# The order of the query tiles in the last attention chunk of a transformer block

## The chip, the cores and the metric

The kernel runs on one core of a Trainium2 chip. The metric is the device time of one execution in microseconds (us), less is better. The engines are called TensorE (PE in the profile; PEld is its weight loading), VectorE (DVE), ScalarE (ACT), GpSimd (POOL) and SyncE (SP, which here only issues DMAs).

## The reference

One layer: causal attention with 16 heads of 32, then a feed forward with the signs of its weights, each followed by a residual sum and a layer norm. Cut to what matters:

```python
# x: (2, 1024, 512) f32
qkv = einsum('bsd,ed->bse', x, w_qkv) + b_qkv            # 3 x 512 columns
scores = q @ k.T / sqrt(32) + causal                      # per batch and head
out = softmax(scores) @ v                                 # back to (2, 1024, 512)
x = layernorm(x + einsum('bsd,ed->bse', out, w_out) + b_out)
hidden = relu(einsum('bsd,hd->bsh', x, sign(up_w)) * up_scale)      # 2048 columns
x = layernorm(x + einsum('bsh,dh->bsd', hidden, sign(down_w)) * down_scale * output_scale)
```

All is float32. Where precision allows fast matmuls, operands are split into a high part and a remainder.

## The kernel before

**Chunks and tiles.** A chunk is one batch with four heads (128 columns); there are 2 x 4 = 8 chunks, done one after the other, and the last is batch 1, heads 12 to 15. Within a chunk the 1024 queries are eight tiles of 128. Because of the causal mask tile i has (i + 1) blocks of 128 keys: tile 0 has 1, tile 7 has 8. Every chunk but the last takes its tiles in the order 0 to 7. The last takes them in the order of the list `LAST`. While one chunk's attention runs, the projections of the next chunk (L568 queries and keys, L605 values) are mixed into TensorE's work; the last chunk has no next one. Instead it has the output projection of batch 1, the signs of the feed forward's weights and the first transposes of the feed forward.

**One tile** goes through these steps for its four heads, which are taken four at a time (tiles 0, 1), two at a time (2, 3) or one at a time (4 to 7):
- scores on TensorE (L861) into one of two double banks of PSUM (`sc`, in the profile `d`)
- on VectorE the mask and the negated maximum of a row: one custom instruction per head and a read of its accumulator (L899), or for four heads at once a sum (L881) and a reduction (L891)
- on ScalarE the exponential with its row sum (L914), on VectorE the reciprocal (L926), on GpSimd the multiplication by it (L932)
- transposes of 128x128 blocks on TensorE (L961), up to four into one bank, and a copy of the bank on ScalarE (L506) or VectorE (L508), whichever the planner takes
- products with the values on TensorE (L988), in one group for one or more tiles, into one bank, and a sum with the value bias on VectorE that writes the chunk's columns into `atT` (L1008)

**Which tiles share a value group.** `attend` puts a tile on a list; if the tile is in `TOGETHER` and is not the chunk's last, the list waits for the next tile, otherwise one group is made of all on the list:

```python
TOGETHER = (0, 1, 3, 4, 6)
...
            apart = i == tiles[-1] or at == 0 and i < NQ // 2
            attend(b, e, i, past, i in TOGETHER and not apart)
            past += i + 1
```

In the last chunk `LAST = [0, 1, 2, 7, 6, 5, 4, 3]` gives the groups 0+1+2, 7, 6+5, 4+3.

**Output and first norm.** When all four chunks of a batch have a tile's columns, `output` multiplies them with `w_out` (L1053, four pairs of matmuls, one per chunk), adds on VectorE the residual row (L1064) and takes statistics (L1068, L1072). The residual row is loaded by SP (`rows<-in_x`) into a single buffer, and GpSimd adds the output bias to it (L1047); the next row's load waits until the sum at L1064 has read it. `normalise` then computes the eight inverse deviations of a batch at once on GpSimd (L1082, L1089) and scales its eight tiles on VectorE (L1097).

**Feed forward.** Four blocks of 512 rows. A block needs its rows transposed (L1122) and split into two parts by ScalarE (L1129) and VectorE (L1134) in `xt`. For each of 16 slices f of the hidden columns: eight up matmuls (L1174), relu on ScalarE (L1185), a cast and a remainder on VectorE (L1191, L1196, `hid`), and down products (L1218) for four row tiles. The signs of the weights are taken on ScalarE (L1148), four pieces of 1 MB for each matrix, from the buffer `raw`, which holds one piece, or for two pieces of the down weights from the space of `atT`. The first block is of batch 0 and needs nothing of the last chunk but its space: the hidden slices lie where probabilities were, and the signed down weights where the last chunk's queries and keys were.

**What sets the order.** The program is a list of tasks with a due place each. A planner in the program (`Plan.schedule`) goes through them with costs written down for each task, takes on each engine the ripe task with the smallest place, and so fixes the order on every engine and the buffer of every tile before the program is built. Due places in the last chunk follow from the list: `past` grows by i + 1 with each tile, scores get `at - EAGER` (12 earlier), values `base - 2`, outputs the tile's own begin plus i + 1 + `LAG` (6). Four single banks of PSUM are shared by transposes, value groups, projections and up matmuls, with a limit for each class (`SHARES`). On the chip each engine keeps the planned order and waits on semaphores.

The line that is changed is read here:

```python
        tiles = list(range(NQ))
        if at + 1 == len(chunks):
            tiles = LAST
```

Of the kernel before, what the change touches and what calls it, by code (L numbers as in the profile page):

```python
# [27 lines left out]


TOGETHER = (0, 1, 3, 4, 6)  # L30
LAST = [0, 1, 2, 7, 6, 5, 4, 3]
HURRY = 6.0
PTB = 60

# [247 lines left out]
def kernel(  # L282
# [1025 lines left out]
    for at, (b, e) in enumerate(chunks):  # L1308
# [4 lines left out]
        if at + 1 == len(chunks):  # L1313
            tiles = LAST
        begin, past = {}, base
# [110 lines left out]
```

## Time and profile before

| | |
|---|---|
| median of 3 runs | 757.22 us (756.72 to 757.74) |
| the profiled execution's own time | 758.0 us |
| its span, first to last instruction | 756.2 us |
| granted TensorE clock, mean | 0.999 |
| attention's last chunk, about | 431 to 498 us of the span |
| feed forward, about | 504 us to the end |
| busy in the stretch 480 to 490 us: TensorE, VectorE, ScalarE | 9.58, 6.57, 6.45 us |

The profile is of one execution. Busy time is the union of an engine's instructions; a matmul's end is modelled. In the table of stretches each row gives for one stretch its length and then the busy time and instruction count of each engine. In a timeline each row gives start, length, engine, line, operation, what it writes and reads, shape and count, and in brackets the idle time before it and what ended that.

### The profile page before, as it was taken

Reading aid. Unit: us, or ns where it says so; the run is one execution under the profiler, and the core shown is the slowest. Engines: PE = TensorE matmul, PEld = TensorE weight load, DVE = VectorE, ACT = ScalarE, POOL = GpSimd, SP = SyncE. Lnnn points to the kernel's source line nnn. Section 1 sums busy time; section 2 is a strip of 40 time slices with the busy share of each in tenths; the row PEclk is TensorE's granted clock in tenths of the full one; section 3 lists DMA queues with packets and bytes.
Section 4 is the critical chain, followed back from the end, with each engine's and each line's share of the span. In section 5 each row is a group of like instructions: output and inputs, shape, how many; then the busy total and the mean of one; then the engine's idle time right before and its main releaser. Section 6 shows DMA issues by size and latency. Waiting matters only on the chain.

```text
span 756.2 us, 15485 instructions
## 1 busy us (share of the span) xinstructions
PE 745.9 (99%) x5890; PEld 576.9 (76%) x5890; DVE 479.5 (63%) x1152; ACT 377.4 (50%) x848; POOL 257.0 (34%) x327
## 2 busy tenths in 40 slices
PE   9999999999999999999999999999999999999996
PEld 5668869769757776886977977668787787778885
DVE  2657787787755766887778769744336337335536
ACT  1448776766742755677676667823222222222210
POOL 2416445445535453554544555521001002002000
PEclk9999999999999999999999999999999999999999
DMA  6576446056454225514505534241001001000101
GB/s 185 129 160 149 120 99 141 28 113 155 126 127 112 56 71 112 120 37 100 126 1 114 126 113 154 84 136 74 1 0 57 0 1 56 0 1 1 56 1 55
DMA packets 38216, 62.35 MB, mean 82 GB/s; under 512 B 6144, under 2 KB 18432, under 8 KB 38144
## 3 DMA queue, kind: packets, MB, share of 16 engines
q1 hardware_dynamic: 36912, 60.85, 31.5%
q8 instruction: 46, 0.75, 0.5%
q10 hardware_dynamic: 1232, 0.53, 0.3%
q14 instruction: 26, 0.21, 0.1%
HBM read 24.66 MB, written 4.19 MB: 38 GB/s over the span
## 4 chain that ended last, share of the span: by engine, by line
PE 93%; DVE 4%; SPq 1%; ACT 1%; DMA 0%; issue 0%; ACTq 0%; DVEq 0%
PE s L961 16%; PE s L1174 15%; PE pd L1218 14%; PE s L568 13%; PE d L861 9%; PE s L988 9%; PE s L1053 7%; PE s L605 7%; PE s L769 1%; SPq L524 1%; PE s L1122 1%; DVE small L1264 1%; DVE atT L1247 1%; DVE d L899 1%; PE s L726 1%; ACT probs L914 1%
## 5 line engine op out<-in xcount | busy, mean ns | idle before, releaser
L932 POOL TENSOR_SCALAR probs<-probs,small 128x128 f32<-128x128 f32 (+7 forms) x256 | 189.1, 749 | 233.1 <-DVE small L926 151.2
L914 ACT ACTIVATE probs<-d,small 128x128 f32<-128x128 f32 (+7 forms) x256 | 189.3, 747 | 47.8 <-DVE small L926 18.7
L899 DVE CUSTOM_DVE_ANT_0 d<-d,mask 128x384 f32<-128x384 f32 (+7 forms) x200 | 173.3, 877 | 26.2 <-PE d L861 23.1
L961 PE MATMUL s<-ident,probs 128*128 128x128 f32 x1152 | 161.4, 273 | 1.1 <-DVE probsT L508 0.7
L961 PEld LDWEIGHTS s<-ident,probs 128*128 128x128 f32 x1152 | 135.5, 140 | 32.9 <-issue 23.3
L506 ACT COPY probsT<-s 128x512 f32<-128x512 f32 (+3 forms) x206 | 100.8, 519 | 116.0 <-PE s L961 111.9
L1174 PE MATMUL s<-xt,stacks 128*128 128x512 f32 x512 | 133.1, 400 | 0.0
L1218 PE MATMUL pd<-stacks,hid 128*128 128x512 f32 (+1 forms) x512 | 131.8, 392 | 0.6 <-DVE hid L1191 0.6
L1185 ACT ACTIVATE hf<-s,ups 128x512 f32<-128x512 f32 x64 | 44.0, 688 | 160.3 <-PE s L1174 158.5
L861 PE MATMUL d<-stacks 128*128 128x512 f32 (+3 forms) x368 | 120.8, 423 | 0.9 <-ACT probs L914 0.9
L568 PE MATMUL s<-xT,wqkv 128*128 128x512 f32 x240 | 118.6, 595 | 0.3 <-DMA wqkv<-in_w_qkvT 0.3
L1174 PEld LDWEIGHTS s<-xt,stacks 128*128 128x128 f32 x512 | 94.3, 188 | 23.8 <-issue 1.0
L1218 PEld LDWEIGHTS pd<-stacks,hid 128*128 128x128 f32 x512 | 92.7, 188 | 22.6 <-DVE hid L1191 1.4
L1191 DVE CAST hid<-hf 128x512 fp32r<-128x512 f32 x64 | 27.4, 428 | 121.7 <-ACT hf L1185 121.7
L508 DVE COPY probsT<-s 128x512 f32<-128x512 f32 (+3 forms) x139 | 81.7, 596 | 22.5 <-PE s L961 18.4
L861 PEld LDWEIGHTS d<-stacks 128*128 128x128 f32 x368 | 59.8, 190 | 35.8 <-issue 20.4
L605 PE MATMUL s<-wqkv,xT 128*128 128x128 f32 x512 | 75.5, 276 | 0.0
L605 PEld LDWEIGHTS s<-wqkv,xT 128*128 128x128 f32 x512 | 67.9, 191 | 6.6 <-issue 5.6
L988 PE MATMUL s<-probsT,v 128*32 128x128 f32 x2304 | 68.9, 274 | 0.1
L988 PEld LDWEIGHTS s<-probsT,v 128*32 128x32 f32 x2304 | 61.2, 110 | 10.2 <-DVE small L926 2.7
L1053 PE MATMUL s<-wout,atT 128*128 128x512 f32 x128 | 63.4, 594 | 0.0
L568 PEld LDWEIGHTS s<-xT,wqkv 128*128 128x128 f32 x240 | 39.5, 190 | 19.3 <-issue 17.8
(71 smaller groups left out, 517.6 us busy)
## 6 DMA issues: line engine op xcount, KB each, us to landing
stacks<-wqkv SPq DMA_DIRECT2D x224, 128.0 KB, 2.4
wqkv<-in_w_qkvT SPq DMA_DIRECT2D x22, 256.0 KB, 3.6
xT<-in_xT SPq DMA_DIRECT2D x16, 256.0 KB, 4.4
rows<-in_x SPq DMA_DIRECT2D x16, 256.0 KB, 2.7
raw<-in_up_wT SPq DMA_DIRECT2D x4, 1024.0 KB, 5.1
out<-atT SPq DMA_DIRECT2D x16, 256.0 KB, 2.0
stacks<-wqkv SPq DMA_DIRECT2D x48, 64.0 KB, 2.0
raw<-in_down_wT SPq DMA_DIRECT2D x2, 1024.0 KB, 5.6
```

The costliest lines, as they stand in the source:

```text
L506: nc.scalar.copy(dst, src)
L568: nc.tensor.matmul(of(ps).rearrange("p a b -> p (a b)"), lhsT=of(w)[:, c, n, :], rhs=of(xt)[:, c, t0 : t0 + TB], start=(c == 0), stop=(c = ...
L605: nc.tensor.matmul(of(ps)[:, t, :], lhsT=of(xt)[:, c, t0 + t * P : t0 + (t + 1) * P], rhs=of(w)[:, c, 2, :], start=(c == 0), stop=(c == NC ...
L861: nc.tensor.matmul(of(sc)[:, at0 : at0 + k1 - k0], lhsT=of(st)[:, 0, u, ts(i, P)], rhs=of(st)[:, 1, u, k0:k1], start=True, stop=True,)
L899: lambda _, j=j, some=some: nc.vector.tensor_tensor_reduce(some(), some(), keys(mask[:, S - N :], 0, N), scale=-1.0, scalar=LARGEST, op0=A ...
L914: lambda _, j=j: nc.scalar.activation(keys(of(pr), j, N), keys(of(sc), j, W), AF.Exp, bias=of(nm)[:, j : j + 1], scale=sign, accum_out=of( ...
L932: lambda _, j=j: nc.gpsimd.tensor_scalar(of(pr)[:, j * N : (j + 1) * N], of(pr)[:, j * N : (j + 1) * N], of(sums)[:, j : j + 1], 1.0, ALU. ...
L961: lambda _, k=k, c=c, tp=tp: nc.tensor.transpose(of(tp)[:, k, :], of(pr)[:, c], ident),
L988: nc.tensor.matmul(of(to)[ts(u, HD), n, :], lhsT=of(v)[:, k, ts(u, HD)], rhs=turned(pt, c + k, 1)[0], start=(k == i), stop=(k == 0),)
L1053: lambda _, c=c: nc.tensor.matmul(bank(py), lhsT=of(a)[:, c, :], rhs=of(wout)[:, c, :], start=(c == 0), stop=(c == NC - 1),),
L1174: lambda _, f=f, c=c, n=n, pu=pu: nc.tensor.matmul(of(pu), lhsT=of(up)[:, f // TPB, c, ts(f % TPB, P)], rhs=of(xt)[:, n, c, :], start=(c = ...
L1218: lambda _: nc.tensor.matmul(of(to)[:, d0:d1], lhsT=of(h)[:, ts(t, P)], rhs=of(dn)[:, f // 4, f % 4, d0:d1], start=(f == 0 and n == 0), st ...
```

## The change

One list of eight numbers, the order in which the last chunk takes its query tiles. The rest of the program text is the same.

```diff
 TOGETHER = (0, 1, 3, 4, 6)
-LAST = [0, 1, 2, 7, 6, 5, 4, 3]
+LAST = [2, 7, 6, 5, 4, 3, 1, 0]
 HURRY = 6.0
```

Three things follow from it through the code above. Tiles 0 and 1 go from the chunk's start to its end. The value groups become 2, 7, 6+5, 4+3+1+0. And all due places of the chunk's tasks change, so the planner gives another order to every engine from the chunk's start on: on TensorE up to the first down products of the feed forward, on VectorE until a little later, on ScalarE, GpSimd and SP in the order of exponentials, signs, row sums and loads.

## The prediction

> **What bounds the kernel now.** I read the page's first two parts, then the chain of waits, then TensorE's own waits, then busy time by stretch. The page's busy line and the chain's summary:
>
> ```profile
> PE 745.9 (99%) x5890; PEld 576.9 (76%) x5890; DVE 479.5 (63%) x1152; ACT 377.4 (50%) x848; POOL 257.0 (34%) x327
> PE 93%; DVE 4%; SPq 1%; ACT 1%; DMA 0%; issue 0%; ACTq 0%; DVEq 0%
> ```
>
> TensorE is nearly always occupied and carries 93% of the chain that ended last. So an order of work can only gain what TensorE now idles, and loses whatever new idle time it makes. The view of TensorE's waits shows how little there is:
>
> ```profile
> PE s L726 <- DVE x L722: 1.0, 1, 1.0
> PE d L861 <- ACT probs L914: 0.9, 2, 0.7
> PE s L961 <- DVE probsT L508: 0.7, 1, 0.7
> PE pd L1218 <- DVE hid L1191: 0.6, 2, 0.3
> PE s L568 <- DMA wqkv<-in_w_qkvT: 0.3, 1, 0.3
> PE s L961 <- DVE xT L1064: 0.3, 1, 0.3
> ```
>
> Of these the change can reach 0.7 (L861, at 450.2), 0.7 (L961, at 477.3) and 0.3 (L961, at 489.1). The first lies at the kernel's start, the two on hid in the second half.
>
> The order of instructions says where the change begins and ends. TensorE's first changed instruction starts at 430.95 (the scores of tile 0 before, of tile 2 after, while 10 of the value projections at L605 are still to come). Its first down product (L1218) starts at 508.75 by the chain; from there to the end the order on TensorE is the same in both kernels. Busy time in that stretch, and in the part of it where tiles 7 to 4 are worked through:
>
> ```profile
> core 0: us, PE busy (x) PEld busy (x) DVE busy (x) ACT busy (x) POOL busy (x), PEclk, DMA share, GB/s
> 430.95:508.75 77.80, 75.95 (x741) 55.03 (x741) 57.20 (x142) 50.21 (x103) 35.90 (x42) 1.00 0.34 111
> 443.07:484.20 41.13, 39.59 (x393) 28.86 (x392) 34.36 (x87) 31.48 (x57) 20.23 (x21) 1.00 0.38 129
> ```
>
> TensorE idles 77.80 - 75.95 = 1.85 us in the whole stretch. In the second, VectorE is busy for 34.36 of 41.13: it is next in line.
>
> **What is moved.** Counted from the two orders, TensorE runs the same instructions between those two points: 32 pairs of output projection, 168 attention transposes, 16 transposes for the feed forward, 48 score matmuls, 408 value matmuls, 10 pairs of value projection, 16 up matmuls. Nothing is added or removed, so the change in span is the change in idle time. The value groups (L988) go from tiles 0+1+2, 7, 6+5, 4+3 (24, 32, 52, 36 pairs) to 2, 7, 6+5, 4+3+1+0 (12, 32, 52, 48). What moves is filler: output projections that can run as soon as a group's columns exist. Before, 12 pairs (tiles 0 to 2, 12 x 0.86 = 10.3 us) become ready at 453 and cover tiles 7 and 6. After, 4 pairs (3.4 us) do, then 4 of tile 7, and 16 pairs are left for the end. In return tile 7's scores start beside the last value projections.
>
> **A ledger through the new order.** I walked TensorE's new order from 430.95 with durations of this profile (start to start): 0.109 a transpose, 0.86 a pair of output projection, 0.47 two score matmuls of 512 columns, value groups at 0.029 a matmul; on the others 1.15 a maximum over 1024 keys on VectorE, 1.11 an exponential of 1024 on ScalarE with its accumulator, 0.48 to 0.60 a copy of 512, 1.03 a normalising multiply of 1024 on GpSimd, 1.8 a sign, 0.1 a hand-over. Where it comes out tight:
> - Scores of tile 6, second head: TensorE is there at 448.5. The bank needs tile 7's last exponential, which stands behind a sign on ScalarE (445.5 to 447.3) and ends at 448.4. Slack 0.1.
> - Values of tile 7: at 453.5, last copy 453.4. Slack 0.1.
> - Tile 7's output projection waits 0.1 for its bank (copy on VectorE ends 457.4).
> - Ahead of values 6+5, around 467: a sign on ScalarE (466.4 to 468.2) again stands among the casts of xt, and VectorE's subtraction and two copies follow one another. Waits 0.35 + 0.25 + 0.25 = 0.85.
> - Tile 3's transposes: 0.3 for a copy queued behind a mask on VectorE (479.4), then 0.45 because GpSimd adds tile 5's residual row (1.28 us) between the normalising multiplies of two heads.
> - Last group, 4+3+1+0: copies done at 491.9, TensorE there at 492.3. No wait; it has one up matmul in front and 10 output pairs with 15 up matmuls behind (12 us), which hide the relu, the hid casts and the down weights' signs.
>
> The sum of idle time is 0.1 + 0.85 + 0.75 = 1.7 us against 1.85: -0.15. The same kind of wait is visible before, in ScalarE's timeline, where a sign between two casts made the 0.75 us gap at 477.3:
>
> ```profile
> 475.21 0.59 ACT L1129 CAST xt<-s 128x512 fp32r<-128x512 f32 x1
> 475.69 1.93 ACT L1148 ACTIVATE stacks<-raw 128x2048 fp32r<-128x2048 f32 x1
> 477.50 0.58 ACT L1129 CAST xt<-s 128x512 fp32r<-128x512 f32 x1
> ```
>
> **What is queued differently behind it.** The residual row has one buffer, so eight loads, GpSimd adds and VectorE sums go in turn. On SP's queue tile 0's load now stands behind the two 1 MB loads of down weights (before: ahead of them); these landed 5.6 and 7.8 us after issue, so the row comes about 9 us after the last output projection, near 516.5, and its sum on VectorE after GpSimd's 1.28. It stands behind the hid casts of f = 4 there, which cannot run before 519.5: cost nothing. Batch 1's normalisation then starts later, and its eight multiplies (L1097, 0.47 each) stand on VectorE in one block of 3.8 us ahead of hid f = 7 (before: 1 + 1 + 6). It starts behind hid 6 at 528.0, so hid 7 is done at 533.5; the down product wants it at 533.6 to 533.9. A wait between 0 and 0.7; I take 0.2. If the cover were gone, TensorE would wait the whole block, 3.8.
>
> Sum: -0.15 + 0.2 = about +0.1. The profiled execution took 758.0, of which 756.2 is span; the median of the runs is 757.22, 0.8 under it. The change of span goes onto the median: 757.22 + 0.1 = **757.3**. About 0.2%, 1.5 us, is what can be told from no change here.
>
> **Bounds.** No new idle and all the old closed: -1.85, 755.4. Above: ten hand-overs have under 0.3 of slack; 0.1 more each is +1.0, 758.3.
>
> One rule would move the lower bound. The Trainium skill, "Perfetto Trace Analysis", section "Identifying the Most-Contended Engine", says that matmul busy time is no measure of TensorE's headroom, since pipelined matmuls hide in it, and asks for the weight-load share instead. By that the stretch (55.03 of 77.80) would leave much more than 1.85 to win. Against it stands a count from this profile: the same instructions at the durations above give 73.9, so at most 75.95 - 73.9 = 2.05 us of the busy time is hidden waiting, and most of that shows right behind the four value groups, which both kernels have. Taken in full it would give 753.3; I leave it 2 in 100, inside the chance of faster.
>
> **Rivals.**
> 1. Slower: VectorE runs out between the first maximum of tile 7 and the columns of 6+5. My ledger gives TensorE 36.8 us there (435.2 to 472.0). VectorE's instructions in it sum to 32.3; the same count for the stretch before gave 33.4 where 34.36 was busy, so 33.3. Its idle time before was 6.6 us by its timeline, 4.1 of that waiting for TensorE and 2.5 for ScalarE. With 2.5 it needs 35.8 and fits; with all 6.6 it needs 39.9, and TensorE starves for 3.1. It decides from 3.5 us of waiting. Time at that price: 757.3 + 3.1 = 760.4; with half, 758.9. For it: only 8 output pairs are left as filler, and ScalarE's signs stand in the chain. Against it: 4.1 of the 6.6 vanish when TensorE is ahead.
> 2. Faster: the old gaps close and the new ones don't open, since tile 7 starts 6 us earlier and the light tiles 1 and 0 end the chunk: 755.4. Against it: the ledger's 0.85 at 467 and 0.75 at 479 to 485.
> 3. Slower, in the feed forward: hid 7 comes late by more than its margin because tile 0's row or the normalisation's statistics slip; the block then costs up to 3.8, 761. For it the margin of 0.1; against it 3 us of slack on the row itself.
>
> **Chances.** Forecast, idle within 1.5 us of now: 0.58. Rival 1: 0.25. Rival 3: 0.07. Rival 2 and the hidden waiting: 0.10. So faster by over 0.2% 0.10, within 0.58, slower 0.32. The range runs from 756.0, two thirds of the way to rival 2, to 759.8, which takes in rival 1 up to four fifths of its price; about 2 in 10 lie outside. The likeliest case's own range is 756.2 to 758.4.
>
> **What would show it.** Right: TensorE idle between 430.95 and the first down product near 1.7 us, with gaps at 467 and between 479 and 485, the first down product within 1 us of 508.75, and the same length from there on. Rival 1: gaps on L961 and L861 between 453 and 472 released by VectorE, and VectorE over 95% busy there. Rival 3: a gap on L1218 released by hid near 534. Rival 2: under 0.4 us idle before the first down product. The prediction is wrong if that idle time is over 3.3 or under 0.4, or if the span moves while it does not.

## The result, and the profile after

The changed kernel takes 755.5 us (median of 12 runs, 754.66 to 756.5); the kernel before, measured beside it, 757.62. The ratio is 0.9971 with a 95% interval of 0.9963 to 0.9979: 2.2 us faster. The forecast was 757.3, no change that can be told, with a range from 756.0; the measured time lies under it, and near the 755.4 of rival 2, which shared a chance of 0.10 with the hidden waiting.

The page's busy line and chain, after:

```profile
PE 745.2 (99%) x5890; PEld 576.6 (76%) x5890; DVE 482.0 (64%) x1158; ACT 376.0 (50%) x843; POOL 256.4 (34%) x327
PE 95%; DVE 4%; ACT 0%; issue 0%; DVEq 0%; ACTq 0%
```

TensorE is busy 0.7 us less for the same 5890 matmuls, in a span that is 2.2 us shorter (754.0 against 756.2). All of TensorE's waits after that the view lists (it lists those over 0.15 us):

```profile
PE s L726 <- DVE x L722: 1.0, 1, 1.0
PE pd L1218 <- DVE hid L1191: 0.6, 2, 0.3
PE s L988 <- issue: 0.4, 1, 0.4
PE s L961 <- DVE xt L1134: 0.2, 1, 0.2
PE d L861 <- ACT probs L914: 0.2, 1, 0.2
```

The 0.9 on L861 is down to 0.2, which lies ahead of the last chunk in both. The 0.7 on L961 behind a copy and the 0.3 behind the residual sum are gone. The only wait longer than a tenth in the changed stretch is 0.2 behind the remainder of `xt`. (The 0.4 on L988 lies before the last chunk too.) Busy time by stretch: tile 7's first scores to the end of the values of 6+5, then the whole changed stretch, from the first changed scores to the first down product:

```profile
core 0: us, PE busy (x) PEld busy (x) DVE busy (x) ACT busy (x) POOL busy (x), PEclk, DMA share, GB/s
434.26:471.11 36.85, 36.64 (x486) 29.68 (x484) 32.42 (x80) 28.98 (x54) 19.04 (x22) 1.00 0.35 115
430.48:506.33 75.85, 75.64 (x743) 55.17 (x742) 57.62 (x143) 48.87 (x99) 34.65 (x42) 1.00 0.33 111
```

The kernel before, between the same two records as the second row:

```profile
430.71:508.59 77.88, 76.03 (x743) 55.11 (x742) 57.31 (x141) 50.45 (x104) 36.03 (x43) 1.00 0.34 110
```

The whole stretch took 75.85 us with 75.85 - 75.64 = 0.21 idle, where the kernel before has 77.88 us with 77.88 - 76.03 = 1.85 idle. (The prediction took its ends, 430.95 and 508.75, from the chain of waits, which enters these two records a little later; the idle time is the same.) So 2.03 of the 2.2 us are won here: 1.64 are idle time, and 0.39 are busy time that became shorter though the matmuls are the same.

Not all of the 2.03 belongs to the order. The values of 6+5 are the same 104 matmuls in both kernels, and from their start to the next scores they took 480.16 to 483.45 before, 3.29 us, and 468.14 to 471.11 after, 2.97 us:

```profile
480.16 3.36 PE L988 MATMUL s<-probsT,v 128*32 128x128 f32 x104
483.45 1.20 PE L861 MATMUL d<-stacks 128*128 128x512 f32 x4
```

```profile
468.14 3.04 PE L988 MATMUL s<-probsT,v 128*32 128x128 f32 x104
471.11 0.56 PE L861 MATMUL d<-stacks 128*128 128x320 f32 x2
```

In every other trace of this case they took 2.97 or 2.98 as well. So the profiled execution of the kernel before halted once inside this group, for 0.31 us: 0.11 of it shows as idle, which no semaphore ended, and 0.20 counts as busy. Without this halt the gain in the stretch is 1.72 us, of which 1.53 are idle time and 0.19 busy time; that still lies in the interval of the runs, 1.6 to 2.8 us.

Ahead of the first changed instruction nothing was changed, and there the two executions drift against each other: the changed one is 1.2 us ahead at 36 us, after a faster start and without a wait of 0.33 for a weight load (L568), and only 0.23 ahead at the first changed instruction (430.48 against 430.71), after its halt of 0.43 on L988 at 244 among others. From the first down product on, the two are equal (247.61 and 247.67).

### The profile page after: what moved, and what is told of

Its sections match the earlier page's. It is cut to its first block, busy times and chain, and to the rows that moved or that the text cites. A ratio compares the mean times of both kernels' runs of the same rounds, so it can differ in the third digit from the quotient of the medians.

```text
span 754.0 us, 15484 instructions
## 1 busy us (share of the span) xinstructions
PE 745.2 (99%) x5890; PEld 576.6 (76%) x5890; DVE 482.0 (64%) x1158; ACT 376.0 (50%) x843; POOL 256.4 (34%) x327
## 4 chain that ended last, share of the span: by engine, by line
PE 95%; DVE 4%; ACT 0%; issue 0%; DVEq 0%; ACTq 0%
PE s L961 16%; PE s L1174 15%; PE pd L1218 14%; PE s L568 14%; PE d L861 9%; PE s L988 9%; PE s L605 8%; PE s L1053 7%; PE s L769 1%; PE s L1122 1%; DVE small L1264 1%; DVE atT L1247 1%; PE d L842 1%; PE s L726 1%; DVE atT L1290 0%; DVE d L899 0%
## 5 line engine op out<-in xcount | busy, mean ns | idle before, releaser
L961 PE MATMUL s<-ident,probs 128*128 128x128 f32 x1152 | 161.8, 273 | 0.2 <-DVE xt L1134 0.2
L961 PEld LDWEIGHTS s<-ident,probs 128*128 128x128 f32 x1152 | 135.3, 140 | 32.8 <-issue 22.0
L506 ACT COPY probsT<-s 128x512 f32<-128x512 f32 (+3 forms) x201 | 98.6, 519 | 108.3 <-PE s L961 104.7
L861 PE MATMUL d<-stacks 128*128 128x512 f32 (+4 forms) x368 | 120.7, 421 | 0.2 <-ACT probs L914 0.2
L568 PE MATMUL s<-xT,wqkv 128*128 128x512 f32 x240 | 118.6, 595 | 0.0
L508 DVE COPY probsT<-s 128x512 f32<-128x512 f32 (+3 forms) x145 | 84.5, 591 | 23.8 <-PE s L961 19.9
L861 PEld LDWEIGHTS d<-stacks 128*128 128x128 f32 x368 | 59.6, 190 | 34.0 <-issue 19.5
L988 PE MATMUL s<-probsT,v 128*32 128x128 f32 x2304 | 68.9, 274 | 0.4 <-issue 0.4
L988 PEld LDWEIGHTS s<-probsT,v 128*32 128x32 f32 x2304 | 61.2, 110 | 9.6 <-DVE small L926 2.4
L568 PEld LDWEIGHTS s<-xT,wqkv 128*128 128x128 f32 x240 | 39.5, 190 | 18.9 <-issue 17.4
```

The source lines that it names most:

```text
L506: nc.scalar.copy(dst, src)
L568: nc.tensor.matmul(of(ps).rearrange("p a b -> p (a b)"), lhsT=of(w)[:, c, n, :], rhs=of(xt)[:, c, t0 : t0 + TB], start=(c == 0), stop=(c = ...
L861: nc.tensor.matmul(of(sc)[:, at0 : at0 + k1 - k0], lhsT=of(st)[:, 0, u, ts(i, P)], rhs=of(st)[:, 1, u, k0:k1], start=True, stop=True,)
L961: lambda _, k=k, c=c, tp=tp: nc.tensor.transpose(of(tp)[:, k, :], of(pr)[:, c], ident),
L988: nc.tensor.matmul(of(to)[ts(u, HD), n, :], lhsT=of(v)[:, k, ts(u, HD)], rhs=turned(pt, c + k, 1)[0], start=(k == i), stop=(k == 0),)
```

## The experiments

Two questions. Which part of the new order closed the three gaps? And why did the ledger find 1.7 us of new idle time where 0.21 came? The column "length" below is from the start of the first scores of the last chunk to the start of the last up matmul, in the profiled execution of each kernel, and "idle" what TensorE idled in it; about 0.6 of that is in every kernel, in the feed forward. The length before has the halt of 0.31 in it.

| kernel | ratio to before (95%) | length | idle |
|---|---|---|---|
| before | 1 | 308.47 | 2.42 |
| changed | 0.9971 (0.9963 to 0.9979) | 306.47 | 0.78 |
| e1: 2, 7, 6, 5, 1, 0, 4, 3 | 1.0009 (1.0000 to 1.0017) | 308.29 | 2.11 |
| e2: 7 first, descending | 0.9999 (0.9990 to 1.0008) | 307.70 | 1.77 |
| e3: only 0 to the end | 0.9991 (0.9983 to 1.0000) | 307.71 | 1.47 |
| e4: before, due place of a sign later | 1.0008 (0.9998 to 1.0018) | 308.91 | 2.43 |
| e5: changed, 0 and 1 exchanged | 0.9975 (0.9964 to 0.9985) | 307.03 | 0.82 |
| e6: changed, 4+3 and 1+0 apart | 0.9969 (0.9957 to 0.9981) | 306.70 | 0.82 |
| e7: before, transposes later | 0.9992 (0.9983 to 1.0000) | 307.77 | 1.70 |
| e8: changed, transposes later | 0.9982 (0.9973 to 0.9990) | 307.18 | 1.28 |
| e9: changed, 2 output pairs short | 0.9967 (0.9955 to 0.9978) | 306.06 | 0.77 |
| e10: changed, 4 pairs short | 0.9963 (0.9949 to 0.9976) | 305.84 | 1.19 |
| e11: before, 4 pairs short | 0.9993 (0.9985 to 1.0002) | 307.75 | 3.54 |
| e12: before, value projections later | 1.0025 (1.0016 to 1.0034) | 309.64 | 2.36 |

**e1, e2, e3: other orders.** Each is one line.

```diff
-LAST = [0, 1, 2, 7, 6, 5, 4, 3]
+LAST = [2, 7, 6, 5, 1, 0, 4, 3]    # e1
+LAST = [7, 6, 5, 4, 3, 2, 1, 0]    # e2
+LAST = [1, 2, 7, 6, 5, 4, 3, 0]    # e3
```

> Order 2, 7, 6, 5, 1, 0, 4, 3: the changed kernel's start (tile 2, then tile 7 beside the last value projections), but tiles 4 and 3 end the chunk as before, in one value group 1+0+4+3. Theory A (tile 7's scores start beside the value projections, VectorE and ScalarE get ahead of TensorE there, and the 0.7 us gap at 450 closes): that gap is gone, the two gaps of 0.75 and 0.3 us near 477 and 489 may stay, 756.0 to 756.6. Theory B (the light tiles 1 and 0 at the end make the gain): the late gaps stay or grow, 757.0 to 757.8. Theory C (any new order shuffles small gaps by chance): anywhere between 755.5 and 759, with gaps at new places.

> Order 7, 6, 5, 4, 3, 2, 1, 0: no light tile at the start at all, so that no output projection of this batch is ready before tile 7's values and tile 7 starts still earlier. Theory A: at least as fast as the changed kernel, 755.0 to 755.8. The forecast's first rival (too little output projection as filler starves TensorE once VectorE is behind): slower than the changed kernel by 1 to 3 us, 756.5 to 758.5, with gaps on transposes and scores released by VectorE between 440 and 455. Theory C: no relation to either.

> Order 1, 2, 7, 6, 5, 4, 3, 0: only tile 0 goes to the end, groups 1+2, 7, 6+5, 4+3+0. Tile 7 starts one light tile (0.4 us of scores) earlier than before, and one light tile ends the chunk. Theory A: half of the gain or less, 756.3 to 757.2, the gap near 450 smaller. Theory B: most of the gain, 755.5 to 756.2, since a light tile is the last. Theory C: no relation.

Measured: e1 758.4 (the kernel before beside them: 757.86), e2 757.79, e3 757.39. In none of the three traces is there the wait at 450; so where tile 7's scores start earlier, this gap closes, as theory A says. But A's times fail: e1, with the changed kernel's start, is not faster than before, and e2 not faster than the changed kernel. TensorE's waits of over 0.15 us in e1's last chunk, from its timeline:

```profile
468.16 1.12 PE L1053 MATMUL s<-wout,atT 128*128 128x512 f32 x2 [0.46 <-ACT probsT L506]
...
485.78 1.06 PE L961 MATMUL s<-ident,probs 128*128 128x128 f32 x8 [0.66 <-DVE probsT L508]
...
487.21 2.84 PE L1053 MATMUL s<-wout,atT 128*128 128x512 f32 x6 [0.37 <-DVE xt L1134]
```

The first gap is gone and three others are there, with 1.49 us as much as the 1.75 before. e2 has one of 0.74 on a transpose, released by GpSimd's normalising multiply, at 464, and two of 0.2; e3 has 0.39 at 477 and two smaller. So e2, with no early filler at all, has the time that the forecast's first rival was given there (756.5 to 758.5) without its mark: TensorE has no gap between 440 and 455. The start alone gives nothing. The three orders ended within 0.1% of before, each with gaps of its own, which fits theory C. e2's trace is 0.77 shorter in the changed part than before, 0.31 of that the halt, while its time is the same; single executions are worth some tenths here.

**e5 and e6: the end of the changed order.**

```diff
+LAST = [2, 7, 6, 5, 4, 3, 0, 1]    # e5
```

```diff
+            cut = at + 1 == len(chunks) and i == 3                            # e6
-            attend(b, e, i, past, i in TOGETHER and not apart)
+            attend(b, e, i, past, i in TOGETHER and not apart and not cut)
```

> Order 2, 7, 6, 5, 4, 3, 0, 1: the changed kernel with its last two tiles exchanged; TensorE's order is the changed kernel's up to tile 3. If the gain lies in the start together with light tiles at the end (theories A and B), this is the changed kernel within 0.1%, 755.2 to 756.0. Theory C (each order makes its own gaps): a difference of 0.3 to 1 us either way, from gaps after 475 only.

> The changed order, but tile 3 no longer waits for the next tile in the last chunk, so the last value group 4+3+1+0 becomes 4+3 and 1+0. Output projections of 4 and 3 are free earlier, and a fifth value group costs about 0.2 us of its own (a group starts and ends 0.2 us slower than its matmuls add up to). If the joint group is part of the gain: 756.0 to 756.7. If only the order is: 755.6 to 755.9, the 0.2 alone.

Measured: 756.46 and 756.05, beside 758.06 of the kernel before; by the ratios 1.9 and 2.4 us faster than before, the changed kernel 2.2. All three intervals overlap widely. So neither the joint group of four tiles nor the order of the last two has a share of the gain that can be told. (e5's profile is 0.56 longer than the changed kernel's. The records are level up to 477, so this comes behind tile 3's transposes, as theory C has it, and hardly any of it is idle time.) What the three have and e1 does not is tiles 4 and 3 ahead of the light ones 1 and 0. With e1 this suggests that start and end work together: the start closes the gap at 450 and the light end keeps the late gaps closed. But e2 also starts with tile 7, has 4 and 3 ahead of 1 and 0, and waits 0.74 at 464, so the two are not enough by themselves. They were not measured as separate shares, since each change of the list also moves everything behind it.

**e4 and e7: what made the gap at 477.** The prediction read it from ScalarE's timeline: a sign between two casts.

```diff
-                    up, up_wT[:, ts(g, TB)], g, base + 6 * g, base + 6 * g + 4,
+                    up, up_wT[:, ts(g, TB)], g, base + 6 * g, base + 6 * g + (14 if g == 3 else 4),    # e4
```

```diff
-            turn(0, pace(base + 20, base + 34, 16), ["w", "hl", "full"])
+            turn(0, pace(base + 28, base + 40, 16), ["w", "hl", "full"])                                # e7, e8
```

> The kernel before with one due place changed: the fourth sign of the up weights gets 10 more, so that ScalarE takes it later than between the two casts at 475 to 478. If each gap has its own cause, the 0.75 us gap at 477 goes and nothing else moves: 756.6 to 757.0, TensorE idle 1.1 us in the chunk instead of 1.85. Theory C: the new order of the rest opens another gap of the same size, 757.3 to 758.

> The kernel before with the feed forward's first transposes due later (from 28 to 40 in the place of 20 to 34), behind the heavy tiles. If the 0.75 us gap at 477 is made by VectorE's queue (a remainder of xt that waits for ScalarE's cast, then a maximum of 640 keys, then the copy that TensorE waits for), the gap goes: idle 1.1 us in the chunk, 756.7 to 757.2. If sign and cast on ScalarE made it, it stays or comes back later: 757.4 to 758. Theory C: other gaps, no relation.

e4 measured 757.94 against 757.86, no gain, and its trace still waits 0.52 at 478.0. But its edit moved the sign by only 0.7 us: it runs from 476.40 to 478.32, still between the casts at 475.14 and 478.20, so e4 does not test the forecast's reading. (Its length in the table holds a wait of 0.35 for a DMA at 430.98, ahead of what it changes.) The chain of waits of the kernel before does (start, length, what):

```profile
474.73 0.58 ACT probsT L506
475.31 0.50 ACT xt L1129
...
475.83 0.69 DVE xt L1134
476.52 0.74 DVE d L899
477.26 0.06 DVE small L899
477.32 0.56 DVE probsT L508
477.88 0.14 issue
478.01 0.85 PE s L961 x6
```

The sign is not in it. TensorE waits for a copy on VectorE that stands behind a maximum of 640 keys, which stands behind the remainder of `xt`, which waited for the first cast. In e4's chain the same pieces follow one another:

```profile
475.25 0.50 ACT xt L1129
...
475.76 0.69 DVE xt L1134
476.46 0.74 DVE d L899
...
477.27 0.60 DVE probsT L508
```

e7 takes cast and remainder out of this place: the gap is gone, the idle time falls by 0.72 (0.11 of it the halt), the time by 0.6 us (0.9992, an interval that ends at 1.0000). By the chain VectorE's queue made this gap, behind ScalarE's first cast, and the forecast's reading of it was wrong: a timeline shows what runs beside a gap, the chain shows what the gap waits for.

**e8: the same edit on the changed kernel.**

> The changed kernel with the same later due places for the feed forward's first transposes. Its only visible gap in the chunk, 0.2 us at 467, is of the same kind. If gaps have single causes: 755.0 to 755.5, at or just under the changed kernel. Theory C: the new order opens gaps elsewhere, 756 to 757.5, as the three other orders did.

Measured 756.85, 1.4 us faster than before and, by ratios whose intervals still touch, 0.8 slower than the changed kernel. The 0.2 at 467 is gone, and the transposes are now late: 0.46 for the first up matmul, which needs `xt`, and 0.24 at 476. Of the expectations theory C's fits, by its size and by its way.

**e12: filler without the earlier scores.**

```diff
+            late = 12 if at + 2 == len(chunks) else 0
-            project(nb, ne, base + lo, base + lo + MID * (STEP - lo), base + HI * STEP)
+            project(nb, ne, base + lo, base + lo + MID * (STEP - lo), base + HI * STEP + late)
```

> The kernel before with the last chunk's value projections due 12 places later, so that some of them are left as filler beside tile 7, while the tiles keep their old order. If the 0.7 us gap at 450 closes for want of filler alone: gap gone, 0.5 to 0.9 us less than before. If it closes only when tile 7's scores come earlier (theory A): the gap stays, or moves, and the time is that of before within 0.4 us.

Measured 759.47 against 757.94. The gap at 450 is gone here as well, so filler beside tile 7 is enough for it and the earlier scores are not needed. The gain of 0.5 to 0.9 that was expected with it did not come, the kernel is 1.9 us slower: 0.66 at 478 and 0.89 at 489.6 are there now, both behind VectorE. Its length is not compared, because four more value projection pairs lie in it.

**e9, e10, e11: does the ledger's TensorE run too fast?** The order on every engine is kept, and TensorE gets less work: two of a tile's four pairs in batch 1's output projection run on 64 of 512 columns. So 448 columns of these tiles lack two of their four products, and the results of these kernels are not the layer's.

```diff
+        thin = b == B - 1 and i in (7,)        # e9; (2, 7) in e10 and e11
...
-                    bank(py),
+                    bank(py)[:, : 64 if thin and c in (1, 2) else D],
                     lhsT=of(a)[:, c, :],
-                    rhs=of(wout)[:, c, :],
+                    rhs=of(wout)[:, c, : 64 if thin and c in (1, 2) else D],
```

> The changed kernel with the same order on every engine, but the second and third pair of tile 7's output projection (batch 1) run on 64 of 512 columns, so the rest of these columns lacks two of its four products. TensorE has 1.0 to 1.5 us less work between the values of tile 7 and those of 6+5. Theory K (the forecast's ledger had the other engines' times right and let TensorE run about 0.8 us too fast, so it counted waits that a TensorE at its real pace does not meet): the waits of the ledger now appear near 467, 0.6 to 1.2 us instead of 0.2, and the time falls by 0.5 us or less, 755.2 to 755.8 where the changed kernel has 755.5. Rival R (the ledger's times for VectorE and ScalarE were too long and they have ample slack): the gap stays near 0.2 and the whole 1.0 to 1.5 is saved, 754.0 to 754.6.

> As the run with tile 7's two short pairs, with tile 2's second and third pair short as well: 2.0 to 3.0 us less TensorE work ahead of the values of 6+5, order unchanged. Theory K: nearly all of the second saving turns into waits between 445 and 470, idle time there 1.5 to 2.5 us, the time 754.8 to 755.6. Rival R: 752.5 to 753.5.

> The kernel before with the same four pairs short (tiles 2 and 7, second and third pair), order unchanged. It already waits 0.7 us at 450 and 0.75 at 477 for other engines. Theory K: TensorE is not what the stretch hangs on near these waits, so most of the 2.0 to 3.0 us turns into longer waits, time at most 1 us less than before. Rival R: 2 us or more less than before.

What a short pair costs is read where nothing behind it waits. In e11 one stands between transposes, and from its start to theirs are 0.17 us:

```profile
459.78 0.33 PE L1054 MATMUL s<-wout,atT 128*128 128x64 f32 x2
459.95 1.37 PE L961 MATMUL s<-ident,probs 128*128 128x128 f32 x8
```

The same pair takes 0.86 in the kernel before (459.53 to 460.39). So by this one place 0.69 us of work is taken away with each pair, 1.38 with two and 2.76 with four, within what was expected. (In e9 the first short pair, with the scores behind it, takes 0.73 where the changed kernel has 1.21, only 0.48 less. But those scores begin at 459.04, and the exponential that frees their bank ended at 458.99, so that time has waiting in it.) The time fell by far less: 0.3 us in e9, 0.6 in e10 (0.9967 and 0.9963 against 0.9971), and 0.5 in e11 (0.9993). The intervals are wider than these falls, but the lengths say the same: 0.41, 0.63 and 0.72 less (0.41 for e11 without the halt in the kernel before). Three quarters or more of the work taken away are given back in waiting. In e10 0.28 of it shows, at 448.2 behind GpSimd's normalising multiply. In the kernel before more of it shows. Its waits around tiles 7 to 5 in e11:

```profile
461.66 0.67 PE L861 MATMUL d<-stacks 128*128 128x512 f32 x2 [0.17 <-ACT probs L914]
...
462.60 1.95 PE L988 MATMUL s<-probsT,v 128*32 128x128 f32 x64 [0.27 <-DVE probsT L508]
...
473.60 0.57 PE L861 MATMUL d<-stacks 128*128 128x320 f32 x2 [0.54 <-ACT probs L914]
```

They are new, 0.98 in sum. In e9 no such wait is listed. From the values of tile 7 to those of 6+5 it needs 14.06 where the changed kernel needs 14.49 (start, length, of the value groups; first the changed kernel, then e9):

```profile
453.65 1.95 PE L988 MATMUL s<-probsT,v 128*32 128x128 f32 x64
...
468.14 3.04 PE L988 MATMUL s<-probsT,v 128*32 128x128 f32 x104
```

```profile
453.20 1.95 PE L988 MATMUL s<-probsT,v 128*32 128x128 f32 x64
...
467.26 3.05 PE L988 MATMUL s<-probsT,v 128*32 128x128 f32 x104
```

Busy time in these two stretches, in the same order:

```profile
453.65:468.14 14.49, 14.28 (x145) 11.38 (x144) 13.29 (x35) 12.43 (x23) 8.68 (x9) 1.00 0.32 108
```

```profile
453.20:467.26 14.06, 13.85 (x145) 11.11 (x144) 13.21 (x35) 12.22 (x22) 8.70 (x9) 1.00 0.36 111
```

Both idle 0.21; in e9 it is two pieces, 0.10 at 459.9 and 0.11 at 466.4, too short for the list of waits. So the stretch is 0.43 shorter for 1.38 less work, and by this price some 0.95 us of waiting lies inside time that counts as busy. Whom TensorE waits for, the chain of e9 says. In the changed kernel the chain runs on TensorE from 452.96 to 463.32. In e9 it runs on other engines from 452.45 to 459.92, most of it on ScalarE, a sign among it, and then enters TensorE with scores:

```profile
455.36 1.66 ACT stacks L1149
...
458.76 1.11 ACT probs L914 x3
459.88 0.04 issue
459.92 0.61 PE d L861 x2
```

So with 1.38 us less work on TensorE it is the other engines, ScalarE above all, that this stretch hangs on up to 459.92. Theory K's times hold, R's (752.5 to 754.6) do not; K's gap of 0.6 to 1.2 at 467 did not show as one. K's other half, that TensorE's own pace is slower than the ledger's, is not tested by these runs.

## Why the prediction was wrong

**The step that failed is the ledger's sum of idle time, 1.7 us, and its comparison with the 1.85 of the kernel before; 0.21 came.** By its terms: 0.1 at tile 7's output projection, measured none; 0.85 at 467, measured 0.20; 0.75 between 479 and 485, measured none above a tenth.

**Why.** The ledger's durations add up to 73.9 us for the stretch, and the prediction itself put 2.05 us of busy time beyond them aside as possible hidden waiting. It then walked TensorE with the bare durations, counted 1.7 us of waits on top of them, and took from these the 1.85 of the kernel before, which lie on top of 75.95 us of busy time. That compares unlike things. As a length the ledger was good: 73.9 + 1.7 = 75.6, measured 75.85. Set against the 77.80 of the kernel before it gives 2.2 us less, which is about what came; part of that is luck, since the waits did not come where the ledger had them. The same holds from tile 7's first scores to the end of the values of 6+5: the ledger gave 36.8 us, of which 0.95 were waits and 35.85 work; measured were 36.85, of which 0.21 idle and 36.64 busy.

So in place of 0.95 of waits the profile has 0.21 idle, and 0.8 more busy time than the ledger had work. Two things can make that, and the runs do not part them. TensorE may be slower than the bare durations, so that it arrives later and finds its banks ready. Or it waits, and the profile counts this as busy, as e9 shows that it can. What e9, e10 and e11 do show is that the stretch is close to level between TensorE and the others: take 1.38 or 2.76 us of its work away and three quarters or more come back as waiting.

**The reading of the gap at 477 was wrong too.** A sign on ScalarE was named; the chain shows VectorE's queue behind the first cast. The ledger put a sign at 467 for the same reason, and there the wait was 0.20 although the sign ran between the two casts as forecast.

**What held.** The count of the moved work, and with it, to within the 0.39 us of busy time, that the change can only move waits. That the change acts between the first changed scores and the first down product, and that nothing moves behind it: 247.61 and 247.67 us. The single row buffer: tile 0's row was added by GpSimd at 514.99, where the prediction had it landing near 516.5 on a clock some 2 us later. The block of eight multiplies (3.74 us at 526.2) stood ahead of hid 7, which was done at 531.5, and no wait came of it: the 0.2 for it should have been 0. Rival 3 did not occur. VectorE's work was put at 33.3 us of 36.8 and measured at 32.42 of 36.85; it waited 4.4, over the 3.5 from which rival 1 was to decide, without starving TensorE, since its work was 0.9 less.

**The bound and the rule about busy time.** The prediction drew on the Trainium skill, "Perfetto Trace Analysis", section "Identifying the Most-Contended Engine": matmul busy time does not measure TensorE's headroom. (The page's reason is that pipelined matmuls look smaller in the trace, and beside the weight-load share it asks for the share of peak FLOPs; it does not speak of waits.) The prediction set this aside, holding the hidden part to be of a kind that both kernels share. The runs agree with the page that a busy share is not work alone: in e9 some 0.95 us of waiting hides in it. Of the gain itself, 0.39 of the 2.03 us lie in busy time, 0.20 of them the halt. By idle time alone the gain would have been bounded at 1.85.

**The chances.** Rival 2 was given 0.10 because the ledger spoke against it, and its own test, under 0.4 us idle before the first down product, came true. By the same mark the prediction had called itself wrong. Taken as a length, the ledger was for rival 2 and not against it.

**What stays open.** Whether the 0.8 us of busy time that the ledger did not have are TensorE's pace or waiting that counts as busy. How much of the gain is start and how much end. Why this order has nearly no gaps: five other orders or placings of the same work (e1, e2, e3, e8, e12) have 0.7 to 1.8 us of them, two with the same tiles 2, 7, 6, 5, 4, 3 in front (e5, e6) have as few. And the 0.19 us of busy time that are left without the halt: with the same matmuls, length less idle in the table runs from 305.7 (changed) to 306.2 (e3), so orders differ by more than that, and the runs do not say why.

## What to carry to other kernels

When a new order is walked by hand against a measured one, compare lengths, or walk the old order in the same way first and compare its waits with the measured ones. Waits counted on top of bare durations cannot be set against idle time from a profile: here 73.9 us of bare durations stood in 75.6 to 76.0 us of busy time. For a gap take the cause from the chain of waits, not from what runs beside it, and where engines are nearly level, expect an edit to close one gap and open another: e1, e2, e3 and e12 lost the gap at 450 and e7 the one at 477, and none of them was faster than before by more than 0.1%. To learn whether an engine holds a stretch, take some of its work away and see how much of it comes back.

## What the runs showed of the hardware that was not expected

A pair of output projection matmuls with 64 in the place of 512 columns took 0.17 us of its 0.86 where nothing waited behind it (e11, 459.78); with scores behind it that waited for ScalarE, 0.28 and 0.43 to their start (e9, 458.76 and 459.49). Waiting of about 0.95 us, by that price, can lie in a stretch (e9, between the values of tile 7 and of 6+5) in which the profile shows TensorE idle for 0.21, no more than with the work still there. And a group of 104 value matmuls that took 2.97 or 2.98 us in thirteen traces took 3.29 in one, with no semaphore behind the halt.
